# A stacked graph network on one Trainium2 core: the sort's transposes in a PSUM bank of their own, the preparation on one bank

## The chip, the cores and the metric

The kernel runs on one core of one Trainium2 chip, in one launch. The metric is the device time in microseconds (us), the median of several runs. Five engines work side by side, each through its own queue in order: TensorE (PE in the profile; its weight loads are shown as PEld), VectorE (DVE), ScalarE (ACT), GpSimd (POOL) and SyncE (SP), which here only issues DMAs. Results of matmuls go to PSUM, which has eight banks of 2 KB in each of 128 partitions.

## The reference

Sixteen batches of a graph with 1024 nodes and 64 channels go through four layers. Each layer normalises its input, computes an update and adds it. The first layer is the costly one: each node's neighbour list is thinned, and for every node and channel three quantiles (0.25, 0.5, 0.75) over the remaining neighbours' values are taken and added up with weights.

```python
ni = neigh.astype(jnp.int32)
rank = jnp.cumsum(ni, axis=-1) - ni
skip = jnp.where(nb > T, (nb + K - 1) // K, 1)
rem = neigh & (sk > 1) & (rank % sk == sk - 1) & mask[:, :, None]
rem = rem | jnp.swapaxes(rem, 1, 2)
nd = jnp.where(rem, 0.0, adj_) > 0
s = jnp.sort(jnp.where(nd[..., None], x[:, None, :, :], jnp.inf), axis=2)
for tau, w in zip(TAUS, WTS):
    pos = tau * jnp.maximum(nv - 1, 0)
    agg = agg + w * (v_lo + frac * (v_hi - v_lo))
y = relu((x + agg) @ W1 + b1) @ W2 + b2
```

The other three layers are a gated update with one gather over the adjacency, a two-layer network with one gather, and an attention whose weights come from the adjacency and two learned vectors, again with one gather.

## The kernel before

Batches are worked on in eight pairs, numbered 0 to 7 here. For each pair there are five kinds of work.

- **Sort** (`sort_begin`, `sort_pair`). Instead of sorting each node's neighbours, the kernel sorts each channel's 1024 values once: 128 partitions hold the 64 channels of two batches, and a bitonic network of 55 steps runs along the row, all on DVE. Each step writes a mask of swaps (L729) and a maximum and a minimum (L736, L737). Four steps' masks (512 KB) go to DRAM as `m_d`. They come back in the opposite order, and the network is run backwards on codes with exclusive-or (L753 to L760), so that every node learns its place. `sort_begin` normalises the input and brings it into channel order with eight PE transposes (L714), whose results ACT copies out (L717). `sort_pair` ends with eight transposes of the codes (L799, copied out at L800), and the result goes to DRAM as `y_d`. The working rows `s4` have three buffers.
- **Preparation** (`prepare`, `neighbours`), for each batch. The adjacency is read row block by row block (`a`, two buffers). Each block is transposed on PE in groups of four (L831), copied out by ACT (L833) and stored as `a_d` for the layers. DVE makes a running count of neighbours (L820, L825), ACT derives from it which neighbours are removed (L854 to L856), and PE puts the thinned adjacency together: groups of up to four 128x128 blocks, three matmuls a block (L875), copied out by ACT (L881) into `ndT`. A last group counts what is left (L885, used at L892). A batch has 16 groups of transposes, 22 groups of blocks and one of counts.
- **Selection** (`weights`, `select`, with `compact` in it). The codes become weight tables (L921), and PE multiplies the thinned adjacency by them (L1045), so that each result word encodes which neighbours of a node lie in a window of the sorted row. ACT copies them out (L1055), DVE takes maxima (first at L1114, L1119), PE transposes (L1101), ACT takes signs (L1103), PE looks values up (L1148), and DVE picks among them (L1156).
- **Extras** (`extras`): the few nodes whose quantiles fall outside the windows are done again, from L1263 to L1319.
- **Layers** (`layers`), for each batch: the rest of the four layers. The gathers (L1409) read `a_d` back in blocks `adjT` (L1402, two buffers for each batch). The attention is a chain of DVE (L1511, L1513, L1519), ACT (L1518, L1524) and PE.

PSUM, in banks. In selection the pools `sp` and `sc` take four banks each, all eight. After selection, `nbp` takes two and extras take six; when extras end, the layers take those six as `lb0` and `lb1`, three for each batch of the pair. `nbp` serves preparation and sort together: every group of theirs is a tile named `pk`, and the two banks go round among them in the order in which the program asks for them. In iteration `pr` of the main loop the program asks in this order: selection of `pr`, extras, layers, then preparation of the next pair, the end of the next pair's sort, and the beginning of the sort of the pair after that. Ahead of the loop it asks for the sort of pair 0, then its preparation, then the beginning of the sort of pair 1.

The order in which instructions stand on each engine is not written by hand. A scheduler sets it when the program is built, from the order of the program, the data dependencies and the buffers: an instruction is put into its engine's queue when its inputs and its buffer are to be had and nothing earlier in the program is ready. So DVE work of the sort, which needs no PSUM between its first and last transposes, can be put between the DVE instructions of any stage. The queues themselves are then fixed. SP's queue carries the loads `a`, `adjT`, `x`, the sort's `m_d` in both directions, `y_d`, `h_d` and the output; ACT issues the stores to `a_d`.

Of the kernel before, what the change touches and what calls it, by code (L numbers as in the profile page):

```python
# [9 lines left out]
F32 = mybir.dt.float32  # L10
# [10 lines left out]
PSUM = bass.MemoryType.PSUM  # L21
DRAM = bass.MemoryType.DRAM

P = 128
# [18 lines left out]
def gnn_stack(ctx, tc, x, adj, nodemask, w, out):  # L43
# [613 lines left out]
    def norm(pool, big, xt, g, name):  # L657

        st = pool.tile([P, g, 6], F32, name=f"{name}_st")
        mv = pool.tile([P, g, 2], F32, name=f"{name}_mv")  # L660
        for t in range(g):
            nc.vector.bn_stats(st[:, t, :], xt[:, t, :])
        for t in range(g):
            nc.vector.bn_aggr(mv[:, t, :], st[:, t, :])
        sd = pool.tile([P, g], F32, name=f"{name}_sd")
        nc.scalar.activation(sd, mv[:, :, 1], AF.Sqrt, bias=eps, scale=1.0)
        rs = pool.tile([P, g], F32, name=f"{name}_rs")
        nc.vector.reciprocal(rs, sd)
        d = big()
        nc.vector.tensor_sub(d, xt, mv[:, :, 0:1].to_broadcast([P, g, C]))  # L670
        h = big()
        nc.vector.scalar_tensor_tensor(
            h, d, 0.0, rs.rearrange("p (g o) -> p g o", o=1).to_broadcast([P, g, C]), op0=ALU.max, op1=ALU.mult
        )
        return h
# [13 lines left out]
    def row4():  # L689
        return so.tile([P, N], F32, name="s4", bufs=3)  # L690

    def sort_begin(pr, nbp):

        def rows():
            return row4().rearrange("p (g c) -> p g c", c=C)

        xt = rows()
        x4 = xt.rearrange("p (t b) c -> p t b c", b=2)
        for b in range(2):
            nc.sync.dma_start(x4[:, :, b, :], x[pr * 2 + b].rearrange("(t p) c -> p t c", p=P))  # L700
        h = norm(so, rows, xt, NT * 2, "so")
        h4 = h.rearrange("p (t b) c -> p t b c", b=2)
        for b in range(2):
            nc.sync.dma_start(h_d[pr * 2 + b], h4[:, :, b, :])
        more_ = so.tile([P, N], U16, name="code").bitcast(BF16)
        nc.scalar.activation(more_, h.rearrange("p g c -> p (g c)"), AF.Sign)
        more_ = more_.rearrange("p (t b c) -> p t b c", b=2, c=C)
        for b in range(2):
            nc.sync.dma_start(p_d[pr * 2 + b], more_[:, :, b, :])
        cur = row4()  # L710
        for q in range(0, NT, 4):
            ph = nbp.tile([P, 4, P], F32, name="pk")
            for t in range(4):
                nc.tensor.transpose(  # L714
                    ph[:, t, :], h[:, 2 * (q + t) : 2 * (q + t) + 2, :].rearrange("p b c -> p (b c)"), ident
                )
            nc.scalar.copy(cur[:, q * P : (q + 4) * P], ph.rearrange("p t n -> p (t n)"))  # L717
        return cur

    def sort_pair(pr, cur, nbp):  # L720

        nxt = row4()
        groups = range(0, len(steps), GROUP)
        for k0 in groups:
            swapped = so.tile([P, GROUP, N // 2], U16, name="swapped", bufs=2)
            for k, (size, j) in enumerate(steps[k0 : k0 + GROUP]):
# [11 lines left out]
                cur, nxt = nxt, cur  # L738
# [55 lines left out]
        nc.scalar.mul(cf, code, -4.0)  # L794
        cn = row4().bitcast(F16)[:, :N].rearrange("p (t k) -> p t k", k=P)
        for q in range(0, NT, 4):
            pc = nbp.tile([P, 4, P], F32, name="pk")
            for t in range(4):
                nc.tensor.transpose(pc[:, t, :], cf[:, (q + t) * P : (q + t + 1) * P], ident)  # L799
            nc.scalar.copy(cn[:, q : q + 4, :], pc)  # L800
# [106 lines left out]
    def weights(b, sb, behind):  # L907

        node = sb.tile([P, NT, 4, C], F16, name="node")
        nc.sync.dma_start(node[:, :, 0, :], y_d[b])
        positive = sb.tile([P, NT, C], BF16, name="positive", bufs=2)
        nc.sync.dma_start(positive, p_d[b])
        for k in range(1, 4):
            nc.vector.tensor_scalar_add(node[:, :, k, :], node[:, :, 0, :], 4.0 * CODE * k)
        wt = {}
        for g in PIECES:
            wt[g] = sb.tile([P, NT, 8, C], F8, name="wt", bufs=len(PIECES) + 2)
            for k in range(0, 8, 4):  # L920
                nc.vector.tensor_scalar(  # L921
                    wt[g][:, :, k : k + 4, :].bitcast(U8), node, 4.0 * (25 + CODE * (8 * g + k)), 4.0 * 26,
                    op0=ALU.add, op1=ALU.min,
                )
        order = ExitStack()
        rows = w_d[b * C : (b + 1) * C]
        for part, d_, w0, n in ((0, 4, 0, 32), (1, 4, 40, 32), (2, 16, 32, 8)):
            src = rows.rearrange("(q d) w e -> d w q e", d=d_)
            to = vtab[:, part].rearrange("p (q d e) -> p q d e", d=d_, e=24)
            for d in range(d_):  # L930
                if behind is not None:
                    order.enter_context(tc.issue_after(behind))
                    behind = None
                nc.sync.dma_start(to[d : d_ * n : d_, :, d, :], src[d, w0 : w0 + n])
        order.close()
        return wt, positive
# [603 lines left out]
    def prepare(pr, nb, nbp):  # L1540

        made = []
        for i in range(2):
            made.append((
                ndp.tile([P, NT, N], F8, name=f"ndT{i}"), ndp.tile([P, NT, 10], F32, name=f"row10{i}"),
                ndp.tile([P, NT, 3], F32, name=f"qb{i}"),
                ndp.tile([P, NT], F32, name=f"qz{i}"),
            ))
            neighbours(pr * 2 + i, *made[i], nb, nbp)
        return made  # L1550

    def side_pools():
        return (
            tc.tile_pool(reuse_waits="tile", name="nb", bufs=1),
            tc.tile_pool(reuse_waits="tile", name="nbp", bufs=2, space=PSUM),
        )

    pairs = B // 2
    nb_, nbp_ = side_pools()
    with nb_ as nb, nbp_ as nbp:  # L1560
        sort_pair(0, sort_begin(0, nbp), nbp)
        made = prepare(0, nb, nbp)
        if pairs > 1:
            cur = sort_begin(1, nbp)
    taken = None
    for pr in range(pairs):
        with tc.tile_pool(reuse_waits="tile", name="keep", bufs=1) as keep:
            aggs = [keep.tile([P, NT, C], F32, name=f"agg{i}") for i in range(2)]
            kept = {
                "flag": [keep.tile([P, NT], U16, name=f"flag{i}") for i in range(2)],  # L1570
                "vx": keep.tile([P, 9], F32, name="vx"),
            }
            with tc.tile_pool(reuse_waits="tile", name="kn", bufs=1) as kn:
                with (
                    tc.tile_pool(reuse_waits="tile", name="sy", bufs=2) as sy,
                    tc.tile_pool(reuse_waits="tile", name="sw", bufs=1) as sw,
                    tc.tile_pool(reuse_waits="tile", name="sg", bufs=2) as sg,
                    tc.tile_pool(reuse_waits="tile", name="sp", bufs=2, space=PSUM) as sp,
                    tc.tile_pool(reuse_waits="tile", name="sc", bufs=2, space=PSUM) as sc,
                ):  # L1580
                    for i in range(2):
                        wt, positive = weights(pr * 2 + i, kn, None if i else taken)
                        select(pr * 2 + i, i, wt, positive, *made[i], aggs[i], kept, sw, sg, sy, sc, sp)
            nb_, nbp_ = side_pools()
            with nb_ as nb, nbp_ as nbp:
                with tc.tile_pool(reuse_waits="tile", name="xs", bufs=1) as xs, tc.tile_pool(reuse_waits="tile", name="xp", bufs=1, space=PSUM) as xp:
                    taken = extras(pr, kept, aggs, xs, xp)
                with (
                    tc.tile_pool(reuse_waits="tile", name="ly0", bufs=1) as ly0,
                    tc.tile_pool(reuse_waits="tile", name="ly1", bufs=1) as ly1,  # L1590
                    tc.tile_pool(reuse_waits="tile", name="lb0", bufs=3, space=PSUM) as lb0,
                    tc.tile_pool(reuse_waits="tile", name="lb1", bufs=3, space=PSUM) as lb1,
                ):
                    for i, (ly, lb) in enumerate(((ly0, lb0), (ly1, lb1))):
                        layers(pr * 2 + i, (pr * 2 + i) % 4, aggs[i], ly, lb)
                    if pr + 1 < pairs:
                        made = prepare(pr + 1, nb, nbp)
                        sort_pair(pr + 1, cur, nbp)
                    if pr + 2 < pairs:
                        cur = sort_begin(pr + 2, nbp)  # L1600
    sorting.close()


# [1 line left out]
    with tc.tile_pool(name="fl", bufs=1) as fl, tc.tile_pool(name="flp", bufs=1, space=PSUM) as flp:  # L1605
        pr = flp.tile([P, P], F32, name="pr")
# [41 lines left out]
```

## Time and profile before

| | us |
|---|---|
| median of 3 runs | 6534.98 (6533.89 to 6546.8) |
| the profiled execution | 6547.95 |
| its span, first to last instruction | 6546.1 |
| first selection matmul (L1045) of pair 0 | 434.3 |
| first selection matmul of pairs 3, 4 | 2731.8, 3506.9 |
| last L1156 of pair 3, last instruction of its extras | 3218.3, 3318.4 |
| last layer instruction on DVE (L1532) of pair 3 | 3524.6 |
| first selection matmul of pair 7, its last L1156 | 5797.5, 6262.7 |

The span consists of a start of 434 us, in which nothing but pair 0's sort and preparation runs, then eight turns of selection, extras and layers; from one pair's first selection matmul to the next takes about 770 us. A stage's end and the next one's beginning overlap by some 20 us. Granted TensorE clock over the span: 0.828.

In the lists of groups each line has the kernel line, engine, operation, tiles (out<-in), shape and count, then busy us and mean ns of one, then the engine's idle time just before them and what ended most of it. In the timeline each line has start and length in us, and in brackets the idle time before it and what ended that.

### The profile page before, as it was taken

Reading aid. Unit: us, or ns where it says so; the run is one execution under the profiler, and the core shown is the slowest. Engines: PE = TensorE matmul, PEld = TensorE weight load, DVE = VectorE, ACT = ScalarE, POOL = GpSimd, SP = SyncE. Lnnn points to the kernel's source line nnn. Section 1 sums busy time; section 2 is a strip of 40 time slices with the busy share of each in tenths; the row PEclk is TensorE's granted clock in tenths of the full one; section 3 lists DMA queues with packets and bytes.
Section 4 is the critical chain, followed back from the end, with each engine's and each line's share of the span. In section 5 each row is a group of like instructions: output and inputs, shape, how many; then the busy total and the mean of one; then the engine's idle time right before and its main releaser. Section 6 shows DMA issues by size and latency. Waiting matters only on the chain.

```text
span 6546.1 us, 112888 instructions
## 1 busy us (share of the span) xinstructions
PE 4538.7 (69%) x45010; PEld 2819.2 (43%) x45010; DVE 5301.1 (81%) x13031; ACT 3545.5 (54%) x4348; POOL 137.5 (2%) x234
## 2 busy tenths in 40 slices
PE   0167858777577776778577775777767876777856
PEld 0145544355434544355443554344543544435532
DVE  7759985999769996899959998599977999586645
ACT  0165655556456556565555565555555655555623
POOL 0000000000000000000000000000000000000000
PEclk9978868788688887888788897888878888888967
DMA  1320135211451124401352114611155013520024
GB/s 56 110 72 33 57 106 177 70 42 49 137 176 39 50 89 141 128 35 51 92 187 75 39 52 118 188 48 51 51 157 150 33 59 89 176 70 16 8 69 126
DMA packets 525639, 568.14 MB, mean 87 GB/s; under 512 B 265004, under 2 KB 414894, under 8 KB 525102
## 3 DMA queue, kind: packets, MB, share of 16 engines
q1 hardware_dynamic: 381472, 476.43, 24.1%
q10 hardware_dynamic: 142862, 82.31, 4.1%
q8 instruction: 355, 5.82, 0.4%
q0 software_dynamic: 768, 2.10, 0.2%
q14 instruction: 182, 1.49, 0.1%
HBM read 376.95 MB, written 183.76 MB: 86 GB/s over the span
## 4 chain that ended last, share of the span: by engine, by line
PE 44%; DVE 23%; ACT 18%; DMA 11%; issue 4%; ACTq 0%; SPq 0%; POOL 0%; DVEq 0%; POOLq 0%
PE comb L1045 17%; PE cand L1148 6%; ACT sign L1103 6%; DMA adjT<-a_d 4%; PE comb L1101 4%; PE bank L1409 4%; DVE y L1119 3%; ACT y L1055 2%; PE comb L1236 2%; DMA a<-in_adj_dram 2%; PE pk L875 2%; DVE att L1519 2%; DVE adjT L1513 2%; DVE cand L1156 2%; DMA a_d<-at 1%
## 5 line engine op out<-in xcount | busy, mean ns | idle before, releaser
L1045 PE MATMUL comb<-wt,ndT 128*128 128x512 fp8e5 x6144 | 1518.2, 404 | 60.3 <-DVE top L1516 29.3
L1055 ACT ACTIVATE y<-comb,qb 128x1024 int16<-128x1024 f32 (+1 forms) x640 | 629.9, 1025 | 954.4 <-PE comb L1045 954.3
L1045 PEld LDWEIGHTS <-ndT 128*128 128x128 fp8e5 x6144 | 617.7, 103 | 804.3 <-issue 207.6
L1119 DVE TENSOR_TENSOR y<-y 128x512 uint16<-128x512 uint16 (+5 forms) x896 | 703.9, 790 | 66.5 <-PE comb L1101 50.8
L1148 PE MATMUL cand<-vtab,sign 128*128 128x48 f16 (+1 forms) x18432 | 680.6, 192 | 71.9 <-DVE agg L1018 29.0
L1148 PEld LDWEIGHTS <-sign 128*128 128x128 fp8e5 x18432 | 648.1, 97 | 143.6 <-issue 51.7
L1101 PE MATMUL comb<-ident_b,y 128*128 128x128 bf16 x4608 | 392.1, 255 | 436.2 <-ACT sign L1103 382.9
L1103 ACT ACTIVATE sign<-comb,half 128x2048 fp8e5<-128x2048 int16 (+1 forms) x384 | 591.6, 1541 | 124.1 <-PE comb L1101 112.1
L1103 ACT ACTIVATE sign<-comb,lower 128x2048 fp8e5<-128x2048 int16 (+1 forms) x384 | 590.9, 1539 | 0.0
L1156 DVE COPY_PREDICATED cand<-w_f,cand 128x256 f32<-128x256 uint16 (+1 forms) x1536 | 529.5, 376 | 70.7 <-PE cand L1148 69.1
L1101 PEld LDWEIGHTS <-y 128*128 128x128 bf16 x4608 | 357.9, 115 | 460.2 <-issue 454.0
L825 DVE TENSOR_TENSOR_SCAN cum<-ni 128x1024 f16<-128x1024 fp8e5 x128 | 292.9, 2294 | 149.3 <-ACT sq L854 131.1
L1409 PE MATMUL bank<-adjT,nd 128*64 128x512 f32 x1024 | 309.2, 662 | 97.0 <-DMA adjT<-a_d 91.7
L833 ACT COPY at<-pk 128x512 f32<-128x512 f32 x256 | 146.7, 586 | 334.5 <-DMA a_d<-at 167.6
L1409 PE MATMUL bank<-att,hs 128*64 128x512 f32 x512 | 206.9, 893 | 165.7 <-ACT hs L1524 164.8
L875 PE MATMUL pk<-ident_b,ni 128*128 128x128 bf16 x1024 | 217.8, 239 | 145.5 <-ACT at L833 80.0
L729 DVE TENSOR_TENSOR swapped<-s 128x512 uint16<-128x512 f32 x440 | 302.0, 686 | 12.2 <-DMA m_d<-swapped 3.9
L736 DVE TENSOR_TENSOR s<-s 128x512 f32<-128x512 f32 (+2 forms) x440 | 288.5, 656 | 0.0
L921 DVE TENSOR_SCALAR wt<-node 128x2048 uint8<-128x2048 f16 x224 | 267.6, 1216 | 25.8 <-PE comb L1236 25.7
L737 DVE TENSOR_TENSOR s<-s 128x512 f32<-128x512 f32 (+2 forms) x440 | 288.4, 655 | 0.0
L875 PE MATMUL pk<-minus_b,rem 128*128 128x128 bf16 x1024 | 219.3, 242 | 88.3 <-ACT rem L856 88.3
L760 DVE TENSOR_TENSOR code<-code,xo 128x1024 uint16<-128x1024 uint16 x360 | 264.2, 734 | 4.6
(300 smaller groups left out, 8065.3 us busy)
## 6 DMA issues: line engine op xcount, KB each, us to landing
adjT<-a_d SPq DMA_DIRECT2D x384, 512.0 KB
a<-in_adj_dram SPq DMA_DIRECT2D x128, 512.0 KB
a_d<-at ACTq DMA_DIRECT2D x256, 256.0 KB
m_d<-swapped SPq DMA_DIRECT2D x104, 512.0 KB
swapped<-m_d SPq DMA_DIRECT2D x104, 512.0 KB
n_d<-nat SPq DMA_DIRECT2D x128, 128.0 KB
x_d<-xr SPq DMA_DIRECT2D x48, 256.0 KB
comb_x<-x_d ACTq DMA_DIRECT2D x24, 512.0 KB
```

Source lines behind the costliest of these rows:

```text
L729: nc.vector.tensor_tensor(side(swapped[:, k, :], j), hi, lo, op=ALU.is_gt)
L736: nc.vector.tensor_tensor(to_lo, lo, hi, op=ALU.max)
L825: nc.vector.tensor_tensor_scan(cum[:, t - t0, :], ni[:, t, :], wide[:, t, pad - 1 : pad - 1 + N], 0.0, op0=ALU.add, op1=ALU.add)
L875: nc.tensor.matmul(pk[:, n % 4, :], lhs, rhs, start=(n % 4 == 0 and m == 0), stop=(m == len(terms) - 1 and last),)
L1045: nc.tensor.matmul(pw[:, e, :], ndT[:, j, t * P : (t + 1) * P], piece[:, j].rearrange("p w c -> p (w c)"), start=(j == 0), stop=(j == NT - 1),
L1055: nc.scalar.activation(y[:, 0, chunks, at : at + words_ * d_].rearrange("p q (w d) -> p q w d", d=d_), by_word[:, : words_ * C].rearrange( ...
L1101: nc.tensor.transpose(pt[:, q - q0, :], y[:, 0, q, :].bitcast(BF16), ident_b)
L1103: nc.scalar.activation(signs[tl][s][:, q0:q1, :], pt.bitcast(I16), AF.Sign, bias=before[s], scale=-1.0, saturate=False,)
L1119: nc.vector.tensor_tensor(v[:, :, :, :n], v[:, :, :, :n], v[:, :, :, n : 2 * n], op=ALU.max)
L1148: nc.tensor.matmul(cand[:, e, at : at + 12 * d_].rearrange("p (d l) -> p d l", l=12), signs[tl][sec][:, chunk, :], tab[:, q, :, half_ * 12 ...
L1156: nc.vector.copy_predicated(v[:, :, :, dst : dst + k], mk.to_broadcast([P, 2, C // 2, k]), v[:, :, :, frm : frm + k])
L1409: nc.tensor.matmul(po[to : to + C, :], lhs, rhs[:, f * HALF : (f + 1) * HALF], start=(j == 0), stop=(j == NT - 1))
```

## The change

A third pool, `sop`, of one PSUM bank is opened beside `nbp`, which shrinks from two banks to one. The sort's groups (L714, L799) are now tiles named `ps` in `sop`; preparation keeps `pk` in `nbp`. The layers' pools stay at three banks each, and the sum stays at eight. No computation is added or removed. Lines up to 1555 keep their numbers.

```diff
-    def sort_begin(pr, nbp):
+    def sort_begin(pr, sop):
...
-            ph = nbp.tile([P, 4, P], F32, name="pk")
+            ph = sop.tile([P, 4, P], F32, name="ps")
...
-    def sort_pair(pr, cur, nbp):
+    def sort_pair(pr, cur, sop):
...
-            pc = nbp.tile([P, 4, P], F32, name="pk")
+            pc = sop.tile([P, 4, P], F32, name="ps")
...
-            tc.tile_pool(reuse_waits="tile", name="nbp", bufs=2, space=PSUM),
+            tc.tile_pool(reuse_waits="tile", name="nbp", bufs=1, space=PSUM),
+            tc.tile_pool(reuse_waits="tile", name="sop", bufs=1, space=PSUM),
...
-    nb_, nbp_ = side_pools()
-    with nb_ as nb, nbp_ as nbp:
-        sort_pair(0, sort_begin(0, nbp), nbp)
+    nb_, nbp_, sop_ = side_pools()
+    with nb_ as nb, nbp_ as nbp, sop_ as sop:
+        sort_pair(0, sort_begin(0, sop), sop)
         made = prepare(0, nb, nbp)
         if pairs > 1:
-            cur = sort_begin(1, nbp)
+            cur = sort_begin(1, sop)
...
-            nb_, nbp_ = side_pools()
-            with nb_ as nb, nbp_ as nbp:
+            nb_, nbp_, sop_ = side_pools()
+            with nb_ as nb, nbp_ as nbp, sop_ as sop:
...
                         made = prepare(pr + 1, nb, nbp)
-                        sort_pair(pr + 1, cur, nbp)
+                        sort_pair(pr + 1, cur, sop)
                     if pr + 2 < pairs:
-                        cur = sort_begin(pr + 2, nbp)
+                        cur = sort_begin(pr + 2, sop)
```

## The prediction

> **What bounds the kernel now.** I read the page's busy times first, then the windows by stage, then the timeline at two hand-overs. A "pair" is two batches; there are eight, 0 to 7. The sort of pair p+1 is DVE work that hides in pair p.
>
> ```profile
> PE 4538.7 (69%) x45010; PEld 2819.2 (43%) x45010; DVE 5301.1 (81%) x13031; ACT 3545.5 (54%) x4348; POOL 137.5 (2%) x234
> ...
> DVE  7759985999769996899959998599977999586645
> ...
> PEclk9978868788688887888788897888878888888967
> ```
>
> DVE is the busiest engine, but at 9s and 5s by turns. The windows (stretch, its length, then busy us and instructions of PE, PEld, DVE, ACT, POOL, clock, DMA share, GB/s) say where: three of the start, then selection, extras and layers of pair 3, then the same of pair 7, which has no next pair to sort or prepare.
>
> ```profile
> 75.00:283.00 208.00, 2.62 (x12) 2.28 (x12) 195.76 (x368) 7.54 (x13) 0.00 (x0) 1.00 0.25 79
> 283.00:434.30 151.30, 76.85 (x662) 60.94 (x660) 59.26 (x119) 92.19 (x128) 6.81 (x15) 0.63 0.41 118
> 2731.80:3218.30 486.50, 375.24 (x4131) 240.06 (x4130) 454.96 (x1105) 273.99 (x324) 4.51 (x7) 0.86 0.17 52
> 3218.30:3318.40 100.10, 52.91 (x774) 46.66 (x773) 79.20 (x175) 63.76 (x68) 5.21 (x11) 0.65 0.39 109
> 3318.40:3506.90 188.50, 139.97 (x726) 65.66 (x724) 120.47 (x344) 105.71 (x153) 7.77 (x10) 0.81 0.60 184
> 5797.50:6262.70 465.20, 367.62 (x4112) 232.99 (x4111) 311.73 (x807) 269.06 (x313) 2.03 (x2) 0.88 0.08 22
> ```
>
> From 75 to 283 us DVE sorts alone; from 283 to 434 PE and ACT prepare alone. Selection keeps DVE at 94% with the sort in it and still takes 465 us without it: the sort's 180 us there cost some 20. Extras and layers leave DVE 89 of 289 us idle.
>
> Why nothing overlaps at the start: preparation's first transposes (times in ns, then first and last start in us), and from the timeline (start, length) the ACT lines ahead of their first copy-out.
>
> ```profile
> L831 PE MATMUL pk<-ident,a x1024: 272/273/477, 282.2 to 5712.2; 128*128 128x128 f32 x171
> ```
>
> ```profile
> 279.27 1.06 ACT L794 ACTIVATE s<-code 128x1024 f32<-128x1024 uint16 x1 [95.32 <-DVE code L757]
> 281.53 0.58 ACT L800 CAST s<-pk 128x512 f16<-128x512 f32 x1 [1.21 <-PE pk L799]
> ...
> 283.32 0.58 ACT L833 COPY at<-pk 128x512 f32<-128x512 f32 x1 [0.35 <-PE pk L831]
> ```
>
> Sort and preparation take their PSUM tiles from one two-bank ring (pk) in the order in which the kernel asks for them. The sort's last two (L799) were asked for first, so preparation, whose adjacency had been in SBUF since 13 us, begins when the sort has ended. In the steady state the order is turned round: the sort's last transposes stand behind all of preparation, and the next pair's first ones (L714) behind those. The timeline of PE, ACT and DVE where pair 4's selection starts:
>
> ```profile
> 3499.25 1.97 PE L714 MATMUL pk<-ident,s 128*128 128x128 f32 x8 [3.48 <-DVE s L672]
> ...
> 3506.94 4.27 PE L1045 MATMUL comb<-wt,ndT 128*128 128x512 fp8e5 x16
> ```
>
> ```profile
> 3502.28 0.57 ACT L717 COPY s<-pk 128x512 f32<-128x512 f32 x1
> ```
>
> ```profile
> 3530.68 1.35 DVE L1114 TENSOR_SCALAR y<-y 128x4608 int16<-128x4608 int16 x1
> ```
>
> Here the next sort is set up as the last thing before the next selection, which starts about 4 us after the copy out of that bank. So all sorting falls into selection and the start of extras, none into layers.
>
> **What the Trainium skill says.** "Perfetto Trace Analysis", section Optimizing Tensor Performance, Matmuls: groups should rotate through PSUM banks so that the copy-out of one overlaps the next. The trace agrees: in preparation (two banks) PE goes on at 0.107 us a matmul from 386.44 to 388.15 us while ACT copies a bank out at 387.86. "PSUM — Partial Sum Buffer", section PSUM bank collisions raise a hardware error: two engines must not be in one bank and quadrant at once; with one bank PE and ACT must therefore take turns. No run here shows that yet. The same page, Engine vs sequencer instructions: matmuls start in program order, so a preparation group that waits for its bank holds the layer matmuls behind it. "Perfetto Trace Analysis", section Optimization Strategy, says that regimes with different contended engines gain from interleaving; the windows above are such regimes.
>
> **The change part by part.** Instruction counts per engine are the same before and after on PE, DVE, POOL and SP; ACT has 11 fewer, table loads among them (1.28 us each, off the bound). What changes is order, and I counted it in the order of the two built programs.
>
> *The start.* Now preparation of pair 0 stands beside the sort. DVE must do 286 us up to the first selection instruction (L1119), as before (290), but before it stood idle for 163 of the 452 us there. Against a full overlap: ACT has the whole preparation of batch 0 ahead of the sort's first copy, 16 copies of 0.586, 24 of 1.15 (L854 to L856), some 22 of 0.4 and 62 DMA issues of about 0.55 us, together 80 us from 12 on, so the sort starts at 105 to 110 instead of 75. From there DVE has 206 us to the sort's end, with the second batch's preparation in it: 316, with stalls of 10 some 325. Then 5 us for L794 to L800, about 10 for y_d out and back (issue 5763.93, reload issued 5769.02 in pair 7), 3 for four DVE lines: first L1045 at 343 to 350 instead of 434.3. I take **-85**; -105 if nothing stalls, -65 if the startup DMAs on ACT's queue stretch.
>
> *Selection.* By count, 304 of the sort's 352 DVE instructions stand in selection before. After it is 304 in pair 0, 249 in pair 1, 200 in pairs 2 to 6, at the same density, so that they run out at about 5/8 of it. From first L1119 to last L1156 a pair takes 456 us, pair 7 takes 427. The last three eighths by instruction count take 179.3 us in pair 3 and 164.3 in pair 7: **-15** for each of pairs 2 to 6, -7 in pair 1, together -82.
>
> *Extras and layers.* From the last L1156 to the next pair's first L1119 the time is 315 us. Summing each row's mean time over the DVE instructions that stand there gives 222 us of work before and 293 after (87 us of sort where there were 18). Sort filler used to find nothing here; now DVE is nearly full. Lower bound: 293 at selection's 94% is 311, that is -4. Upper bound: cut at L1296, L1318, L1452, L1472, L1506, L921, and taking in each piece the larger of the old time and the new work, plus 2 or 3: 40+65+64+34+35+66+33 = 337, that is +22. The single bank adds to that. A transpose group is 0.66 to 0.9 us of PE and 0.585 of ACT, a pk group 12 x 0.107 and up to 0.6; these now add instead of overlapping. In the new PE order 411 of 656 groups follow the previous one with no other matmul between, 51 a pair, so at most 51 x 0.6 = 31 us of new PE idleness; PE is idle for 96 of the 289 us of these two stages, which hides more than half. 14 more us can appear (+36). SP also gets some 8 stores of m_d (512 KB) amid the adjT loads, each waiting for DVE with adjT queued behind it, at a DMA share of 0.60; two adjT buffers per layer cover most. Against all this, selection no longer waits for L714. I take **+15** for each of pairs 0 to 5, range -4 to +36.
>
> *The end.* Pair 6 prepares on one bank but has no sort in its extras, pair 7 has neither: 0.
>
> Sum on the profiled span: 6546.1 - 85 - 82 + 6 x 15 = 6469; with the 1.9 us around the span 6471. The profiled run (6547.95) lies 13 us above the median of 6534.98, so the forecast is 6458, 1.2% faster.
>
> **Rivals.**
> - *Good filling.* The sort fills DVE gaps as smoothly as in selection, extras and layers cost nothing more, PE's bubbles fall into its idle time. For: the filler is always ready. Against: the layers are a chain over PE, ACT and DMA, and each sort instruction (0.69 us) can stand in front of a chain step. -85 - 82 + 0 = -167: 6368.
> - *The single bank and a full DVE lengthen the layers (slower).* Place: last L1156 to next L1119. Price: 40 us a pair, 240 in all, against -82 and a start of only -65: +93, 6628. It decides from +28 a pair at my other values. For: DVE work of 293 in a 315 us stretch that was never tighter than 94%, back-to-back single-bank groups ahead of the extras' cand matmuls. Against: most PE groups in the layers have layer matmuls between them.
> - *The start does not move.* ACT's 62 issues and the startup DMA chain keep preparation from overlapping: start -10, then -82 + 90: about 6533.
>
> **Chances.** The likeliest 0.50, its own range 6395 to 6520; good filling 0.20; slower 0.22; unmoved start 0.08. A measurement of this kernel tells 0.2% (13 us) from no change. Faster 0.68, same 0.07, slower 0.25. The range takes most of good filling and the lower part of the slower case: 6375 to 6580.
>
> **What would show it.** First L1045 at 330 to 370 us and L831 starting near 15 us: the start. Pairs 2 to 6 at 441 us from first L1119 to last L1156, and sort rows inside layers: the move. 330 us from there to the next L1119, with a DVE share above 0.85 in layers: the price. L831 and L875 waiting longer for L833 and L881: the bank. I am wrong if that last stretch passes 343 us, or if DVE in the start waits on preparation for more than 30 us.

## The result and the profile after

The changed kernel takes 6585.01 us (median of 4 runs, 6570.76 to 6591.27) against 6536.67 us for the kernel before (4 runs). The ratio is 1.0068, with a 95% interval of 1.0048 to 1.0088: slower by 0.7%, where 1.2% faster was forecast. The profiled execution of after took 6570.76 us, 14 us under its median, with a span of 6569.0 us; that of before lies 11 us above the median of its four runs. The two spans therefore differ by 23 us and the medians by 48 us. The stages below are compared within the two profiled executions.

The page of after, its busy times and two rows of the 40 slices:

```profile
PE 4625.6 (70%) x45010; PEld 2887.0 (44%) x45010; DVE 5341.1 (81%) x13031; ACT 3532.2 (54%) x4337; POOL 159.1 (2%) x234
...
DVE  6999989996889778997789977898688986576655
...
PEclk8588878888778977889688886888867888878967
```

Before, DVE's row fell to 5 in four of the turns; here it does so only from the hand-over to pair 7 on. It is filled more evenly, as the change lets it be. DVE executes as many instructions as before (13031) and is busy 40 us longer, and the span is longer all the same. So a more even DVE is not by itself a gain.

The windows of after, for the sort's part of the start and then for selection, extras, layers to the next L1045, and from there to the next L1119, of pair 3 (columns as in the prediction: stretch, length, busy us and instructions of PE, PEld, DVE, ACT, POOL, clock, DMA share, GB/s):

```profile
109.00:336.50 227.50, 45.31 (x328) 34.19 (x328) 213.05 (x398) 50.67 (x72) 10.85 (x6) 0.50 0.34 105
...
2736.50:3181.70 445.20, 348.97 (x4032) 229.57 (x4032) 366.68 (x965) 264.35 (x309) 3.84 (x7) 0.88 0.15 42
3181.70:3296.40 114.70, 59.44 (x678) 50.31 (x679) 95.66 (x218) 64.00 (x66) 4.80 (x8) 0.56 0.47 133
3296.40:3488.00 191.60, 140.81 (x814) 68.61 (x813) 167.21 (x393) 98.64 (x147) 10.98 (x13) 0.81 0.58 186
3488.00:3521.60 33.60, 22.02 (x106) 8.77 (x104) 31.99 (x49) 13.80 (x22) 0.00 (x0) 0.86 0.16 47
```

At the start PE and ACT now prepare while DVE sorts: DVE is busy for 213 of 227.5 us there. The instructions of the two lines that mark this in after (times of one in ns, then first and last start in us), one view for each line:

```profile
L831 PE MATMUL pk<-ident,a x1024: 272/327/477, 6.7 to 5785.7; 128*128 128x128 f32 x171
```

```profile
L1045 PE MATMUL comb<-wt,ndT x6144: 376/379/634, 353.2 to 6248.4; 128*128 128x512 fp8e5 x199
```

Preparation's first transpose starts at 6.7 us instead of 282.2, the first selection matmul at 353.2 instead of 434.3. In the turn of pair 3, the stage to look at is extras, which were the window of 100.10 us shown before. They last 114.70 us now, with 95.66 us of DVE work in place of 79.20. DVE's idle time in extras is 19 us, and it was 21 us: the added work did not go into idle time, and the stage is longer by about as much. By stage, from the trace:

| us | before | after | difference |
|---|---|---|---|
| start to first L1119 | 452.4 | 371.4 | -81 |
| first L1119 to last L1156, sum of 8 pairs | 3615.5 | 3575.1 | -40 |
| last L1156 to the next pair's first L1119, sum of 7 | 2194.8 | 2354.5 | +160 |
| last L1156 of pair 7 to the end | 283.3 | 268.2 | -15 |
| span | 6546.1 | 6569.0 | +23 |

The last stage runs neither sort nor preparation, and its length differs even where nothing in it was changed (275.5 us in the run `start_own` below, which has the loop of before); no gain is read from it.

The lists of groups show the single bank. First before, then after: lines of preparation, with busy us and mean ns of one, then idle time ahead of them and what ended it:

```profile
L875 PE MATMUL pk<-ident_b,ni 128*128 128x128 bf16 x1024 | 217.8, 239 | 145.5 <-ACT at L833 80.0 <-ACT ndT L881 64.9
L831 PE MATMUL pk<-ident,a 128*128 128x128 f32 x1024 | 190.4, 330 | 86.8 <-DMA a<-in_adj_dram 59.7 <-ACT at L833 25.9
L881 ACT ACTIVATE ndT<-pk 128x512 fp8e5<-128x512 f32 (+3 forms) x352 | 158.0, 475 | 101.2 <-PE pk L875 96.5
```

```profile
L875 PE MATMUL pk<-ident_b,ni 128*128 128x128 bf16 x1024 | 252.7, 261 | 185.1 <-ACT ndT L881 175.3 <-ACT at L833 9.7
L831 PE MATMUL pk<-ident,a 128*128 128x128 f32 x1024 | 219.1, 345 | 180.3 <-ACT at L833 116.6 <-DMA a<-in_adj_dram 53.1 <-ACT ndT L881 5.9
L881 ACT ACTIVATE ndT<-pk 128x512 fp8e5<-128x512 f32 (+3 forms) x352 | 167.9, 477 | 282.2 <-PE pk L875 280.1
```

PE's waits for ACT's copies at these two lines rise from 171 to 308 us in all: L875's wait for L881 from 64.9 to 175.3 us and L831's for L833 from 25.9 to 116.6, while L875's for L833 falls from 80.0 to 9.7. ACT's copy L881 waits longer as well, mostly for PE (101.2 to 282.2 us): the two take turns. The timeline of PE in after shows it at the very start (start, length, in brackets the idle time before it and what ended that):

```profile
8.53 1.12 PE L831 MATMUL pk<-ident,a 128*128 128x128 f32 x4 [0.68 <-ACT at L833]
10.32 1.11 PE L831 MATMUL pk<-ident,a 128*128 128x128 f32 x4 [0.68 <-ACT at L833]
```

Four transposes, then 0.68 us for the copy-out, then the next four; in `start_own` below, with two banks, twelve follow each other without a gap at that place:

```profile
7.64 2.85 PE L831 MATMUL pk<-ident,a 128*128 128x128 f32 x12
```

One pair's preparation, from its first L831 to its last L881, grows from 248 to 296 us (means of pairs 1 to 7). Whether that wait or the filled DVE makes the turn longer cannot be told from these rows; the experiments are about that.

### The profile page after: what moved, and what is told of

It reads as the page before. It is cut to its first block, busy times and chain, and to the rows that moved or that the text cites. A ratio compares the mean times of both kernels' runs of the same rounds, so it can differ in the third digit from the quotient of the medians.

```text
span 6569.0 us, 112811 instructions
## 1 busy us (share of the span) xinstructions
PE 4625.6 (70%) x45010; PEld 2887.0 (44%) x45010; DVE 5341.1 (81%) x13031; ACT 3532.2 (54%) x4337; POOL 159.1 (2%) x234
## 5 line engine op out<-in xcount | busy, mean ns | idle before, releaser
L1045 PE MATMUL comb<-wt,ndT 128*128 128x512 fp8e5 x6144 | 1500.9, 400 | 60.0 <-DVE wt L921 26.6
L1045 PEld LDWEIGHTS <-ndT 128*128 128x128 fp8e5 x6144 | 613.8, 103 | 783.4 <-issue 183.8
L1119 DVE TENSOR_TENSOR y<-y 128x512 uint16<-128x512 uint16 (+5 forms) x896 | 706.4, 791 | 158.6 <-PE comb L1101 104.7
L1148 PE MATMUL cand<-vtab,sign 128*128 128x48 f16 (+1 forms) x18432 | 700.9, 194 | 83.7 <-DVE agg L1018 36.6
L1148 PEld LDWEIGHTS <-sign 128*128 128x128 fp8e5 x18432 | 665.5, 98 | 155.4 <-issue 55.8
L1156 DVE COPY_PREDICATED cand<-w_f,cand 128x256 f32<-128x256 uint16 (+1 forms) x1536 | 540.1, 378 | 147.9 <-PE cand L1148 143.7
L875 PE MATMUL pk<-ident_b,ni 128*128 128x128 bf16 x1024 | 252.7, 261 | 185.1 <-ACT ndT L881 175.3
L831 PE MATMUL pk<-ident,a 128*128 128x128 f32 x1024 | 219.1, 345 | 180.3 <-ACT at L833 116.6
L833 ACT COPY at<-pk 128x512 f32<-128x512 f32 x256 | 149.8, 585 | 356.1 <-PE pk L831 246.8
L1114 DVE TENSOR_SCALAR y<-y 128x4608 int16<-128x4608 int16 x128 | 173.7, 1357 | 186.4 <-ACT y L1055 185.9
L881 ACT ACTIVATE ndT<-pk 128x512 fp8e5<-128x512 f32 (+3 forms) x352 | 167.9, 477 | 282.2 <-PE pk L875 280.1
L875 PE MATMUL pk<-minus_b,rem 128*128 128x128 bf16 x1024 | 259.4, 268 | 83.8 <-ACT rem L856 83.5
```

The source lines that it names most:

```text
L875: nc.tensor.matmul(pk[:, n % 4, :], lhs, rhs, start=(n % 4 == 0 and m == 0), stop=(m == len(terms) - 1 and last),)
L1045: nc.tensor.matmul(pw[:, e, :], ndT[:, j, t * P : (t + 1) * P], piece[:, j].rearrange("p w c -> p (w c)"), start=(j == 0), stop=(j == NT - 1),
L1119: nc.vector.tensor_tensor(v[:, :, :, :n], v[:, :, :, :n], v[:, :, :, n : 2 * n], op=ALU.max)
L1148: nc.tensor.matmul(cand[:, e, at : at + 12 * d_].rearrange("p (d l) -> p d l", l=12), signs[tl][sec][:, chunk, :], tab[:, q, :, half_ * 12 ...
L1156: nc.vector.copy_predicated(v[:, :, :, dst : dst + k], mk.to_broadcast([P, 2, C // 2, k]), v[:, :, :, frm : frm + k])
```

## The experiments

Two theories were set against each other. **The sort**: DVE work that now falls into extras and layers stands in front of steps of their chains. **The bank**: preparation on one bank becomes too slow and holds up the next selection. In what follows "the stretch" is the time from a pair's last L1156 to the next pair's first L1119, as the mean of pairs 1 to 5 (before 314.2, after 342.5 us), and "selection" is the time from first L1119 to last L1156, as the mean of pairs 2 to 5 (456.5, and 446.9 us). Both are read from one profiled execution of each kernel. Three kernels with the same loop (before, and `start_own` and `start_wide` below) have stretches of 314.2, 314.0 and 313.6 us.

### One part alone: one bank, and an own bank at the start only

`one_bank` is the kernel before with

```diff
-            tc.tile_pool(reuse_waits="tile", name="nbp", bufs=2, space=PSUM),
+            tc.tile_pool(reuse_waits="tile", name="nbp", bufs=1, space=PSUM),
```

> Only the preparation's bank is taken away: sort and preparation share a ring of one bank, and the sort's DVE instructions stand where they stood before (304 in selection, 44 in extras, none in layers). The changed kernel needs 27 us a pair more than before from the last L1156 to the next first L1119. If the single bank causes it (bank theory), this kernel shows 25 us a pair more there, with preparation near 295 us instead of 245, and is 2.5% slower (about 6700). If the sort's work on a full DVE causes it (DVE theory), that stretch stays within 8 us of 315 and the whole within 1% of before.

`start_own` is the kernel before with a third bank for the sort ahead of the loop only; the loop is untouched:

```diff
-    with nb_ as nb, nbp_ as nbp:
-        sort_pair(0, sort_begin(0, nbp), nbp)
+    with nb_ as nb, nbp_ as nbp, tc.tile_pool(reuse_waits="tile", name="sop", bufs=1, space=PSUM) as sop:
+        sort_pair(0, sort_begin(0, sop), sop)
...
-            cur = sort_begin(1, nbp)
+            cur = sort_begin(1, sop)
```

> The sort gets its own bank only ahead of the main loop, beside two banks for preparation; the loop is as before. Both theories: the start loses 80 to 90 us (first L1045 near 350), everything later as before, so 6455 (ratio 0.987).

Measured: `one_bank` 6652.14 us, ratio 1.0175 (1.0158 to 1.0192). `start_own` 6440.04 us, ratio 0.9839 (0.9817 to 0.9862). In `one_bank` the first L1045 is at 467.8 us, 33 us later than before, preparation takes 295 us a pair, and the stretch is 326.9 us: +12.7 us a pair for the bank while the sort stays where it was. Neither theory's number came: the bank theory had asked for 25 us and 6700, the other for a stretch within 8 us of 315. In `start_own` the first L1045 is at 340.3 us (-94) and all later stages are those of before (stretch 314.0 us). The gain of the change's start is thus to be had without any of its price: this version beats both kernels.

### The sort's own bank with two banks for preparation, and its control

To give preparation two banks and the sort one, two banks must be taken from elsewhere: the extras' transposes (tile `tr`) go through one bank twice in place of two banks once, and the layers of the second batch get two banks. `own_and_two` is after with that; `control_five` is before with the same banks taken away (five for extras and layers).

```diff
+            for q0 in range(0, NQ, 8):
+                pt = xp.tile([P, 512], F32, name="tr").bitcast(BF16).rearrange("p (q n) -> p q n", n=P)
...
-                    tc.tile_pool(reuse_waits="tile", name="lb1", bufs=3, space=PSUM) as lb1,
+                    tc.tile_pool(reuse_waits="tile", name="lb1", bufs=2, space=PSUM) as lb1,
```

and in `own_and_two` alone

```diff
-            tc.tile_pool(reuse_waits="tile", name="nbp", bufs=1, space=PSUM),
+            tc.tile_pool(reuse_waits="tile", name="nbp", bufs=2, space=PSUM),
```

> As the changed kernel, but preparation keeps two banks; paid for by a one-bank transpose tile in extras and two banks for the second batch's layers. The sort still stands early (44 in extras, 109 in layers). Bank theory: the stretch from last L1156 to next L1119 goes back to about 315 to 320, preparation to 245, and the whole to 6400 to 6430. DVE theory: it stays near 340 and the whole near 6560, apart from what the control for the two lost banks shows.

> The kernel before with only the two lost banks of the other run (one-bank transpose tile in extras, two banks for the second batch's layers), no bank for the sort. Both theories: extras 3 to 6 us a pair longer for the split transposes, layers 0 to 5, so 0 to 1.2% slower than before (6540 to 6615).

Measured: `own_and_two` 6563.27 us, ratio 1.0037 (1.0022 to 1.0051); `control_five` 6568.99 us, ratio 1.0058 (1.0041 to 1.0075) (its start is that of before, with the first L1045 at 434.8 us). The stretch is 345.1 us in `own_and_two` and 319.8 us in the control. With two banks for preparation (267 us a pair, and L875 waits 44.0 us for L881 in place of after's 175.3) the early sort still costs 25.3 us a pair. So the single bank is not needed for the loss. Selection is 445.0 us against 453.9 us in the control. The control's windows of pair 3 (extras; layers to the next L1045; from there to the next L1119):

```profile
3225.60:3330.20 104.60, 55.54 (x775) 47.64 (x774) 81.77 (x184) 65.60 (x74) 4.74 (x10) 0.62 0.38 104
3330.20:3516.20 186.00, 140.02 (x714) 66.76 (x714) 114.60 (x325) 98.82 (x147) 6.22 (x10) 0.79 0.59 181
3516.20:3547.80 31.60, 20.99 (x107) 8.20 (x106) 31.52 (x47) 14.12 (x22) 0.00 (x0) 0.90 0.20 59
```

### The early sort held until extras are over

`held` is after, with the beginning of the next sort released only by the last DVE instruction of the extras (L1318), which is kept as `kept["done"]`; `held_two` is `own_and_two` with the same line.

```diff
-                        cur = sort_begin(pr + 2, sop)
+                        with tc.issue_after(kept["done"]):
+                            cur = sort_begin(pr + 2, sop)
```

> The changed kernel, with the sort of the pair after next kept behind the last DVE instruction of extras: 0 sort instructions in extras instead of 56, 96 in layers, 232 in selection. DVE theory (extra sort work in extras is paid one for one, in layers it is mostly hidden): extras fall from 115 to about 95 us, layers stay within 5 us of 192, the stretch from last L1156 to next L1119 is near 327 and the whole near 6520. Bank theory (extras are long because preparation has one bank): extras stay above 108.

> The version with the own sort bank and two preparation banks, with the early sort held until the extras are over, as in the run held, which had one preparation bank. Compared with own_and_two (last L1156 of a pair to the next pair's first L1119 345 us in pairs 1 to 5) and with the control of the same banks without the early sort (320 us). If it is the sort's place in extras, ahead of the chain of extras and preparation, that costs, the extras fall back to some 105 us, preparation stays near 265 us and no longer gates, and the stretch falls to 328 to 334 us: 11 to 17 us less in each of six pairs, time 6460 to 6500. If it is the volume of DVE work in the stretch, wherever it stands, the stretch stays at 340 us or more and the time within 30 us of 6563. If the single bank was what kept the held version at 335 us, the layers from the end of extras to the next L1045 fall from 224 to below 205 us; if not, they stay above 215 us with two banks as well.

Measured: `held` 6564.99 us, ratio 1.0043 (1.0034 to 1.0051); `held_two` 6472.34 us, ratio 0.9911 (0.9888 to 0.9934). The same three windows of pair 3, first of `own_and_two`, then of `held_two`, then of `held`:

```profile
3185.00:3304.00 119.00, 59.98 (x802) 51.50 (x801) 101.79 (x224) 71.01 (x85) 9.80 (x13) 0.63 0.48 135
3304.00:3480.00 176.00, 128.31 (x666) 61.78 (x666) 154.71 (x371) 88.19 (x128) 6.49 (x8) 0.78 0.56 182
3480.00:3531.00 51.00, 35.38 (x157) 14.00 (x156) 50.32 (x81) 21.44 (x31) 0.00 (x0) 0.70 0.27 87
```

```profile
3139.10:3238.50 99.40, 51.15 (x776) 43.63 (x775) 66.34 (x134) 65.09 (x75) 3.77 (x11) 0.66 0.38 108
3238.50:3407.70 169.20, 126.33 (x695) 62.68 (x696) 154.49 (x397) 95.52 (x139) 7.42 (x10) 0.83 0.63 209
3407.70:3456.90 49.20, 28.81 (x156) 11.59 (x155) 49.02 (x77) 22.31 (x31) 0.00 (x0) 0.85 0.23 73
```

```profile
3162.90:3254.10 91.20, 47.81 (x612) 41.52 (x613) 60.67 (x127) 56.43 (x54) 4.79 (x8) 0.59 0.46 131
3254.10:3479.70 225.60, 154.86 (x901) 76.89 (x900) 201.90 (x480) 111.85 (x167) 10.05 (x13) 0.79 0.53 171
3479.70:3497.60 17.90, 14.96 (x84) 7.00 (x84) 17.87 (x21) 7.54 (x13) 0.00 (x0) 0.89 0.14 42
```

With two banks, holding the sort shortens extras by 20 us while DVE has 35 us less to do there; the DVE work of the second window is the same to 0.2 us, and that window is 7 us shorter. The stretch falls to 317.8 us, which is 2 us under the control: the 25 us a pair of the early sort are gone. Extras are 6 us shorter than the control's and the rest of the stretch is 4 us longer, so the 56 us of sort that still stand in the layers cost little. With one bank extras fall even further, to 91.20 us, but the layers give it back: the window after them is 225.60 us where after has 191.60, preparation takes 320 us, and its last L881 ends 12.5 us ahead of the next L1045 (28 us in after, 56 us before). The stretch is 335.2 us. In `held` the extras came as the sort theory said; its layers (within 5 us of 192) and its time (near 6520) did not. `held_two`'s time lies where the place theory put it and its stretch 10 us below; its layers, far below 205 us, say that the single bank is what kept `held` long. One thing limits the reading: held back, the sort also did 43 us more of its work in selection (135 us in place of 92), so place and amount in the stretch changed together. DVE is busy for 307 us of the stretch in `own_and_two` and for 270 in `held_two`. At the half us per us that `fill_layers_2` shows below, these 37 us by themselves would make 18 of the 27 us between the two runs (an estimate). The fill runs hold place and amount apart, but for a smaller amount, 34 us; how the 27 us divide is open.

The stretch in us, by these two factors (in brackets selection):

| | sort late, as before | early | early, held behind extras |
|---|---|---|---|
| two banks | 314.2 (456.5); with five other banks 319.8 (453.9) | 345.1 (445.0), five other banks | 317.8 (455.0), five other banks |
| one bank | 326.9 (455.7) | 342.5 (446.9) | 335.2 (450.7) |

### How much DVE work extras and layers take

The three fill runs add independent DVE operations on a tile that nothing uses (maximum over 128x128 f32, 287 to 292 ns each); the outputs are computed as before. They stand on `start_own`. In `fill_extras` 120 of them follow the extras in the program (the lines below); in `fill_layers` the same 120 are asked for after the layers and held behind the extras' last DVE instruction; `fill_layers_2` has 240 there.

```diff
+                    junk = xs.tile([P, 128], F32, name="junk")
+                    nc.vector.memset(junk, 0.0)
+                    for _ in range(120):
+                        nc.vector.tensor_tensor(junk, junk, junk, op=ALU.max)
```

> The kernel with its own bank for the sort at the start alone (6440), with 120 small DVE operations a pair on a tile that nothing else uses, asked for after extras; 95 of them stand within extras, 25 behind. They cost DVE time only, no bank, no ACT, no PE, no DMA. DVE theory: the stretch from last L1156 to next L1119 grows by at least 0.7 of their busy time. Bank or transfer theory: by less than 0.3 of it, since DVE is idle for 20 us of extras and 68 of layers.

> The same 120 operations, all behind extras, in the layers. DVE theory: the stretch grows by at most 0.4 of their busy time, since layers leave DVE idle for 68 of 188 us. Chain theory (any instruction ahead of a layer step delays the chain): by 0.7 or more.

> The 120 idle-tile DVE operations in the layers doubled to 240: about 68 us of DVE work a pair where 34 us cost nothing (6435). No bank, no DMA, no ACT and no PE in it. Ceiling theory (from the last L1156 to the next first L1119 DVE takes about 255 us of work in 311 us; what goes beyond costs 0.7 us or more each): the stretch grows by about 24 us to 335, the whole to 6590 to 6630. Theory of the sort's side costs (its DMAs, its ACT copies, its place between chain steps): 68 us still nearly free, under 6480.

Measured: `fill_extras` 6568.62 us (1.0057, 1.0039 to 1.0075), `fill_layers` 6435.31 us (0.9841, 0.9817 to 0.9865), `fill_layers_2` 6519.03 us (0.9975, 0.9968 to 0.9982). Against `start_own` that is +129, -5 and +79 us. Windows over the whole stretch of pair 3, of these three in that order:

```profile
3180.00:3510.50 330.50, 212.59 (x1594) 123.66 (x1592) 246.82 (x672) 180.35 (x238) 12.49 (x21) 0.76 0.46 141
```

```profile
3109.30:3426.00 316.70, 210.78 (x1592) 120.75 (x1592) 253.81 (x673) 179.50 (x237) 9.67 (x20) 0.76 0.47 147
```

```profile
3151.10:3477.70 326.60, 213.77 (x1592) 119.73 (x1592) 280.44 (x792) 176.45 (x235) 12.37 (x20) 0.75 0.48 142
```

The first two have nearly the same DVE work in the stretch (246.82 and 253.81 us), and as means of pairs 1 to 5 the stretch is 332.3 and 311.0 us (`start_own` 314.0). The place of 34 us of filler decides over 21 us. In front it costs 18 us, 0.53 of its busy time, which is neither theory's number; behind, it costs nothing, as the DVE theory said. In front it does not even lengthen extras (97 us); the time is lost behind them. When extras end, 64 of the next preparation's 128 transposes (L831) are over in place of 80, and 26 sort instructions have stood in extras in place of 42. Preparation takes 265 in place of 248 us, with the same 56 to 58 us from its end to the next L1045. So the filler displaced preparation and some sort. That the next selection then waits on preparation fits this, but was not tried by itself. The filler is also asked for ahead of preparation, where the early sort is asked for last; how well the one stands for the other is not shown.

The doubled filler in the layers costs 14 us of stretch for 27 us more DVE work. So there is a limit on the amount too, with an average slope of a half between 254 and 280 us of DVE work. Where it begins is not clear: `held_two` had 270 us at no cost, `layers_own` below loses 10 us at 255. Neither theory's number for `fill_layers_2` was met; it fell between them.

### Two more versions

`layers_own` is `start_own` with the sort's bank in the layers as well (not in extras), taken from the second batch's layers; `start_wide` gives the start four banks for preparation and two for the sort.

```diff
+                    tc.tile_pool(reuse_waits="tile", name="lb1", bufs=2, space=PSUM) as lb1,
+                    tc.tile_pool(reuse_waits="tile", name="sop", bufs=1, space=PSUM) as sop,
```

> Own bank for the sort at the start and in the layers, not in extras; preparation keeps two banks; the second batch's layers have two. No sort in extras, 63 sort instructions in layers, 279 in selection. DVE theory: extras near 90 to 95, layers 190 to 200, selection 453, about 6400 to 6440. If sort work in layers is paid in full as well (chain theory), the stretch from last L1156 to next L1119 is 335 or more and the whole 6540.

> The kernel with its own bank for the sort at the start alone, there with four banks for preparation and two for the sort. The start with one bank for preparation takes 353 us to the first L1045, with two 340. If banks still limit it, 325 to 335 and the whole 6425 to 6435; if DVE and ACT limit it, within 4 us of 340 and the whole within 0.2% of 6440.

Measured: `layers_own` 6477.61 us (0.9910, 0.9883 to 0.9938): extras 95 us, stretch 324.4 us, selection 451.1 us, so it loses 38 us to `start_own`. Its time lies between the numbers of the two theories. The stretch of the runs, cut where extras end (means of pairs 1 to 5 in us; the last column counts how many of the next pair's 128 transposes are over then, 64 being the first batch's):

| | extras | rest | stretch | DVE busy in it | transposes |
|---|---|---|---|---|---|
| before | 98.3 | 215.9 | 314.2 | 225 | 76 to 80 |
| `start_own` | 98.8 | 215.2 | 314.0 | 225 | 80 |
| `one_bank` | 102.0 | 225.0 | 326.9 | 225 | 64 |
| after | 115.4 | 227.1 | 342.5 | 295 | 64 |
| `control_five` | 104.4 | 215.4 | 319.8 | 227 | 80 to 83 |
| `own_and_two` | 118.3 | 226.8 | 345.1 | 307 | 96 |
| `held` | 91.7 | 243.5 | 335.2 | 280 | 64 |
| `held_two` | 98.5 | 219.3 | 317.8 | 270 | 80 |
| `layers_own` | 94.7 | 229.7 | 324.4 | 255 | 64 |
| `fill_extras` | 97.1 | 235.1 | 332.3 | 247 | 64 |
| `fill_layers` | 98.5 | 212.6 | 311.0 | 253 | 79 to 80 |
| `fill_layers_2` | 98.7 | 226.4 | 325.2 | 280 | 79 to 80 |

The three windows of pair 3 in `layers_own`:

```profile
3148.30:3242.80 94.50, 48.71 (x712) 42.34 (x712) 60.29 (x127) 61.70 (x64) 2.71 (x9) 0.64 0.39 107
3242.80:3420.50 177.70, 135.22 (x772) 68.16 (x769) 145.87 (x381) 97.64 (x145) 9.36 (x12) 0.83 0.62 196
3420.50:3469.60 49.10, 30.04 (x157) 11.97 (x156) 48.99 (x77) 22.48 (x31) 0.00 (x0) 0.82 0.24 73
```

In `layers_own` the extras are 4 us shorter than in `start_own` and the rest is 14.5 us longer. The bank taken from the second batch's layers is no ready reason: `control_five` takes it too, and there the rest is as before, while extras, with the split transposes that `layers_own` does not have, are 6 us longer. So the 48 us of sort that now stand beside the layers were not free here, or not together with that bank. The last column points to preparation. With 64 transposes over, the rest took 225 us or more in every run; with about 80 it took 213 to 219, but for `fill_layers_2` with its doubled filler. `own_and_two`, with 96, has 226.8 all the same, at 307 us of DVE work. No run changed preparation's progress alone, so this is a link that was seen and not shown as a cause.

`start_wide` takes 6435.46 us (0.9840, 0.9818 to 0.9862), first L1045 at 338.8 us: no further gain. What is left of the start is DVE's; the window of `start_own` from the sort's start to the first L1045 shows DVE busy for 219 of 235 us:

```profile
105.00:340.30 235.30, 40.29 (x328) 32.42 (x329) 218.97 (x435) 52.55 (x75) 11.77 (x6) 0.52 0.32 102
```

## Why the prediction was wrong

The forecast put the profiled span 77 us under that of before, and it came out 23 us over. Of these 100 us some 70 lie in extras and layers, 42 in selection and 4 in the start; the last stage, put at 0, gave 15 back.

**The start: right.** L831 starts at 6.7 us, the sort at 109, the first L1045 is at 353.2 (3 us past the 343 to 350 given) and the first L1119 comes 81 us earlier for the -85 forecast. The bound was read rightly: the ring's order held preparation up, and with it gone DVE sets the length. The rival "the start does not move" is out. The single bank takes 13 us of this gain (353.2 against 340.3 us in `start_own`); at the start the forecast had counted nothing for it. Two readings under the sum were loose. Ahead of the first L1119 DVE is busy for 305 of 452 us before, not 290, and so idle for 147, not 163. And 80 us of ACT work from 12 us on end at 92, not at 105 to 110; that the sort did start at 109 owes something to luck.

**Selection: right in kind, half in size.** Pairs 2 to 6 gained 5, 15, 11, 7 and 6 us in place of 15 each, -40 in all for -82. The step that failed is the reference: pair 7's last three eighths stood for "without sort". But pair 7 has no preparation to begin under its last eighth, and the others have (in pair 3 it begins 16 us ahead of the last L1156), which is the likely reason; it was not tried. By count of L1119, pair 3's eighths five to eight took 46.7, 52.8, 46.7 and 79.8 us before and 43.4, 45.9, 46.2 and 79.4 us after, where pair 7 had 72.6 us in the last. So only the fifth and sixth gain. Nor does the amount of sort in selection alone set its length: with 175 us of it selection takes 454 us in `control_five`, with 135 us 455 in `held_two`, with 151 us 451 in `layers_own` and with 92 us 445 in `own_and_two`.

**Extras and layers: the term that turned the sign.** +15 a pair was taken; +25 on average came (6, 27, 31, 25, 28 and 31 us in pairs 0 to 5, and 12 in pair 6, for which nothing was counted and where `one_bank`, with no early sort, has 15): +160 for +90. "330 us from there to the next L1119" became 342.5, just short of the 343 us named as the bound of being wrong. What was mis-sized was the filling. The step laid old time and new work side by side piece by piece and let the work sink into each piece's idle time. In extras it did not: 16.5 us more DVE work came with 14.6 us more length in pair 3. The upper bound's two pieces for extras add up to 105 us; 115.4 came, where 98.3 were before. Its five pieces behind them, 232 us, were wide enough for the 227.1 measured. So after's +28 of pairs 1 to 5 are 17 in extras and 11 behind them. Holding that work back from extras, with two banks, took the whole loss of the stretch away, though it also took 37 us of DVE work out of the stretch. "DVE share above 0.85 in layers" held (167.21 of 191.60 us is 0.87).

**The single bank: priced rightly alone, but it does not add.** It was given 14 us at most. Alone it costs 12.7 us; on top of the early sort 342.5 against 345.1 us, which with the five other banks' 5.6 us taken off (on the assumption that these add) is 3; with the sort held behind extras 335.2 against 317.8, or 23 by the same subtraction. That fits two chains side by side, of which the later one ends the stretch: extras and the layers' steps behind the sort's work on DVE, and preparation taking turns on its bank. No run separates the two chains. Each alone keeps the stretch long, so removing the sort from extras (`held`) or giving the bank back (`own_and_two`) gains 7 and 3 us, and doing both gains 30. Matmuls start and complete in program order ("PSUM — Partial Sum Buffer" in the Trainium skill, section Engine vs sequencer instructions). By this a group that waits for its bank would hold back what is behind it on PE, which is a likely link between the two, but no run took it alone.

**The rivals.** The slower rival named the place, the two parts and the threshold of +28 a pair; with +28 in pairs 1 to 5 it is what happened, at two thirds of the price a pair and with a start that gained more than it allowed, so at 6585 us in place of 6628. Its weight on a full DVE is supported only in part: in the layers 56 us of sort cost 4 us behind extras in `held_two`, 48 us of it came with 14.5 us in `layers_own`, and the limit on amount has a slope of a half. Good filling is out for extras, and holds behind them only in part: for `fill_layers` fully, for `held_two` nearly, for `layers_own` not.

**What stays open.** Adding what the parts measured alone gives for after 314 + 13 (bank) + some 8 for 17 us more sort in extras (at the half us per us of `fill_extras`) + some 8 for 60 us in layers (between the two layer fills): 343, an estimate that happens to meet 342.5. The same sum gives about 336 for `own_and_two`, which took 345.1. That the sum meets after is therefore luck. How after's 28 us divide between the bank and the early sort is not settled, nor how much of the early sort's part is its place and how much the amount of DVE work. What is shown is that each part alone lengthens the stretch, and that without the single bank and with the sort held behind extras it is back at the control's.

## What to carry to other kernels

Give a stream a buffer of its own where a shared ring's order in fact serialises it with another (the start here: -97 us in `start_own`), and leave the ring alone where the streams already overlap. Filler from another stage was free here only behind the short chain of extras and up to some amount: hold it there, and find the limit by adding idle operations, since the share of idle time on the page did not tell it. Look also at how far the work for the next stage has come when the short chain ends. A stage used as a reference for "without X" must run the same companions as the stage it stands for.

## What the hardware showed that was not expected

- Place as well as amount: 34 us of DVE filler cost 18 us of the stretch ahead of preparation and nothing behind the extras; another 120 operations there (27 us more DVE busy time) cost 14. "Perfetto Trace Analysis" in the Trainium skill, section Optimization Strategy, says that interleaving regimes may improve performance; here it did at the start (-97 us in `start_own`), and in the loop it was free at best, where the filler stood behind the extras.
- Two losses that overlap: one bank 12.7 us, early sort 25.3 us, both together 28.3 us a pair.
- The granted clock in extras of pair 3 was 0.56 in after, 0.54 to 0.59 in the windows with one preparation bank, and 0.61 to 0.69 in those with two. Each window holds other amounts of PE work, and which way the two are linked was not tried. A lower clock alone does not explain after's long extras: `one_bank` has 0.54 there and extras of 101.3 us, after 0.56 and 114.7.
